# Ordering the neighbour counts of a graph network: permuting matmuls replaced by indirect stores to HBM

## The chip, the cores and the metric

The kernel runs on one core of one Trainium2 chip. The metric is the device time of one launch in microseconds (us). "Batch" below means one of the 32 independent graphs of the input. The engines are called as the profile calls them: PE (TensorE; PEld is its weight load), DVE (VectorE), ACT (ScalarE), POOL (GpSimd) and SP (SyncE, which here only starts transfers).

## The reference

There are 32 graphs of 512 nodes with 64 features. Four graph layers follow each other, and each is `x = layernorm(x + layer(x, adj))`: a normalized product with the adjacency matrix, a Chebyshev filter of order four, a layer of hyperbolic pair distances, and a last layer, the only one that the change touches:

```python
def _dilate_adj(adj, mask):                       # layer 3
    adj_ = jnp.where(eye[None], 1.0, adj)
    nb = (adj_ > 0) & (~eye)[None]
    m = nb.sum(-1)
    rank = jnp.cumsum(nb, axis=-1) - 1            # running count of neighbours in a row
    skip = jnp.where(m > 10, (m + 1) // 2, 1)
    removed = nb & do_dil[..., None] & ((rank + 1) % skip[..., None] == 0)
    rem = removed | jnp.swapaxes(removed, 1, 2)
    return jnp.where(rem, 0.0, adj_)

agg = _weighted_nanquantile_agg(x, adj_d > 0)     # quantiles 0.25, 0.5, 0.75 over each node's neighbours
out = x + agg
y = relu(out @ W1 + b1) @ W2 + b2
```

For each node and each feature the values of the remaining neighbours are sorted, and three quantiles of them are summed with weights.

## The kernel before

The kernel has two paths. The fast one, which runs here, is good for the degrees that such graphs have; a second, `dense_layer3`, runs after it only if a flag says that a degree was out of bounds.

**Lanes.** The fast path does each batch in lanes: `front` (load of the adjacency matrix, its transpose `AT`, layers 0 and 1), `pairs` and `tail` (layer 2), `graph` (which neighbours remain, and in which order), `gather` (the k-th neighbour of every node is fetched by a product of the features with a one-hot matrix), `sort` and `head` (sorting networks of min and max on the fetched values, tiles `SB` and `SH`), and for every pair of batches the dense layer and the store of the result.

**Order.** Nothing runs while it is recorded. Each operation goes through `seq.op` with an engine, a planned duration and its dependences. `Order.issue` then plans all batches at once and writes out one list for each engine, in which lanes of several batches are interleaved; an engine runs its list strictly in that order and waits where an operand is not there. Which ready operation goes next is decided by a due time: a period of 80 planned us times the batch number plus a share, which goes through five knots for each lane (`STAGES`); `STAY` is the advantage that a matmul has on PE if its shape is that of the one before it. Where the plan leaves PE idle for more than 0.3 us, `issue` puts in `stay_active` matmuls (lines 1579 and 1580) whose results nobody reads, one for every 0.11 us.

**The graph lane.** `graph` makes the 0/1 matrix `nbT` of neighbours, counts them, forms running counts with a product of `nbT` and `UC`, marks the removed neighbours in `v`, and puts the remaining ones (with the diagonal) into `V`, 512 x 512, four tiles of 128 rows. ACT writes `V` from PSUM and sums its rows at the same time (`accum_out`), which gives the degrees `m3`, kept in `M3`. `order` ranks the nodes by degree: a key of degree and node number, compared with all keys by ACT (`Sign` with a row sum `sg`), gives the rank `rk`, and `spot`, an integer form of it, is kept for the fetches at the end. Then come the steps that the change replaces:

- `perm`: DVE makes four one-hot tiles of 128 x 512 from the ranks, with the even ranks in the first half of the columns and the odd ones in the second (`iotap`).
- `VP`: 16 matmuls with 512 columns, `V` by `perm`, put the columns of `V` in rank order; ACT copies four tiles.
- `slot`: 10 matmuls with 512 columns, `UC` by `VP`, make the running counts down each column; ACT copies four tiles. `slot` says for each neighbour and each ranked node the place of that neighbour (1, 3, 5, ... for those that are there); the gather lane compares it with constants on DVE to get its one-hot tiles `gather_oh`.
- Four more matmuls, `onesP` by `VP`, give the degrees along the columns, from which `dist` and `OHM` are made.

The pool `gm` holds one buffer for each tag: `perm` takes the buffer of `nbT`, and `VP` that of `v`. The lane `graph` has one PSUM bank.

**The way back.** At the end of a pair of batches the results are stored to `ranked` in HBM by SP and fetched in node order by POOL, four indirect transfers of 32 KB for each batch (`fetch`, line 582, into the tile that the profile calls `tail_x`).

**Helpers.** Most operations are recorded by helpers, so many groups of the profile have one line: `tt` 514, `ts` 518, `stt` 521 and `cp` 524 on DVE, `gtt` 537 and `gts` 541 on POOL, `rsqrt` 813 on POOL, `act` 550, `mm` 569 and `tr` 574 on PE, `dma` 578 on SP. The tile names (`graph_perm`, `pairs_L`) carry the lane.

Of the kernel before, what the change touches and what calls it, by code (L numbers as in the profile page):

```python
# [9 lines left out]
F16 = mybir.dt.float16  # L10
BF16 = mybir.dt.bfloat16
I32 = mybir.dt.int32
# [8 lines left out]
P = 128  # L21
# [218 lines left out]
class Order:  # L240
# [4 lines left out]
    ENGINES = ("PE", "DVE", "ACT", "POOL", "SP")  # L245
    HOP = 0.05
    LATE = 0.08
    STAY = 58.8

    def __init__(self, nc, tc):  # L250
        self.nc, self.tc = nc, tc
# [218 lines left out]
def tile_adj_resnorm(ctx: ExitStack, tc: tile.TileContext, x, adj, nodemask, w1k, b1k, att_w, att_b,  # L470
# [45 lines left out]
    def ts(out, a, s1, s2, op0, op1=None):  # L516
        kw = {} if op1 is None else {"op1": op1}
        vec(lambda: nc.vector.tensor_scalar(out, a, s1, s2, op0=op0, **kw), out, [a], True, (s1, s2))  # L518
# [24 lines left out]
    def act(out, a, f, bias=None, scale=1.0, accum_out=None, after=None):  # L543
        sc = [x for x in (bias, scale) if isinstance(x, bass.AP)]
        kw = {k: v for k, v in (("bias", bias), ("accum_out", accum_out)) if v is not None}
        n = width(out)
        table = "exp" if f in (AF.Ln, AF.Exp) else "sig" if f in (AF.Sigmoid, AF.Tanh) else None
        near = 0.06 if a.space == PSUM else 0.1
        seq.op("ACT", near + n * 0.83e-3 + 0.09 * len(sc) + (0.09 if accum_out is not None else 0.0),
             0.1, lambda: nc.scalar.activation(out, a, f, scale=scale, **kw), [out, accum_out], [a, after] + sc, table)  # L550
# [7 lines left out]
    def mm(out, w, a, start, stop, pair=False, opens=None):  # L558

        n, m = width(a), width(w)  # L560
        if a.dtype == F32:

            t = 0.88e-3 * n if pair else 2 * max(0.9e-3 * m, 0.93e-3 * n)
        else:
            t = max(0.035, n * (0.25e-3 if m == D else 0.455e-3))
        def go():
            if opens is not None:
                seq.open = opens
            return nc.tensor.matmul(out, w, a, start=start, stop=stop)  # L569

        seq.op("PE", t, 0.16, go, [out], [w, a], (64 if w.ap[0][1] <= 64 else 128, 64 if m <= 64 else 128))
# [5 lines left out]
    def dma(out, a):  # L577
        return seq.op("SP", 0.06, 4.0, lambda: nc.sync.dma_start(out, a), [out], [a])

    def fetch(out, rows, at, stored):  # L580

# [202 lines left out]
    bias1 = parts3(b1f, "bias1")  # L784
    xs = dram.tile([B, N, D], F32, name="xs")
    ranked = [dram.tile([N, D], F32, name=f"ranked{b}") for b in range(B)]
    M3 = const.tile([P, B, T], F32, name="M3")

    def diag(a):
# [8 lines left out]
    def col(name):  # L798
        return seq.tile(pools["small"], [P, T], F32, name, 2)
# [96 lines left out]
    def graph(nm, AT, m3, res):  # L896

        gm = pools["gm"]
        nbT = seq.tile(gm, [P, T, N], F16, "nbT", 1)
        ts(nbT, AT, 0.0, None, op0=OP.is_gt)  # L900
        tt(diag(nbT), diag(nbT), identb.unsqueeze(1).to_broadcast([P, T, P]), op=OP.is_gt)
        m = bank()[:, :T]
        for t in range(T):
            for k in range(T):
                mm(m[:, t:t + 1], nbT[:, k, t * P:(t + 1) * P], onesP[:, 0:1], start=(k == 0), stop=(k == T - 1))
        mi = seq.tile(pools["small"], [P, T], I32, "mi", 2)
        ts(mi, m, 1.0, None, op0=OP.add)
# [18 lines left out]
        V = seq.tile(gm, [P, T, N], F16, "V", 1)  # L926
        for t in range(T):
            pt = bank()
            tb = slice(t * P, (t + 1) * P)
            mm(pt, identb, v[:, t, :], start=True, stop=False)  # L930
            for k in range(T):
                kb = slice(k * P, (k + 1) * P)
                mm(pt[:, kb], v[:, k, tb], identb, start=False, stop=False)
                mm(pt[:, kb], nbT[:, k, tb], identb, start=False, stop=(k == T - 1 and t < T - 1))
                if k == t:
                    mm(pt[:, kb], identb, identb, start=False, stop=(t == T - 1))
            act(V[:, t, :], pt, AF.Relu, accum_out=m3[:, t:t + 1])
        res["V"] = V

    def order(b, res):  # L940

        gm = pools["gm"]
        V = res["V"]
        key = col("key")
        stt(key, M3[:, b, :], float(N), iotr, op0=OP.mult, op1=OP.add)
        pt = bank()
        for t in range(T):
            tr(pt[:, t * P:(t + 1) * P], key[:, t:t + 1].to_broadcast([P, P]), identf)
        keyh = col("keyh")
        ts(keyh, key, -0.5, None, op0=OP.add)  # L950
        sg = col("sg")
        for t in range(T):
            junk = seq.tile(gm, [P, N], F16, "junk", 1)
            act(junk, pt, AF.Sign, bias=keyh[:, t:t + 1], scale=-1.0, accum_out=sg[:, t:t + 1])
        rk = col("rk")
# [12 lines left out]
        perm = seq.tile(gm, [P, T, N], F16, "perm", 1, "nbT")  # L968
        for t in range(T):
            ts(perm[:, t, :], iotap, rk[:, t:t + 1], None, op0=OP.is_equal)  # L970
        VP = seq.tile(gm, [P, T, N], F16, "VP", 1, "v")
        for j in range(T):
            pt = bank()
            for t in range(T):
                mm(pt, V[:, t, j * P:(j + 1) * P], perm[:, t, :], start=(t == 0), stop=(t == T - 1))
            act(VP[:, j, :], pt, AF.Copy)
        slot = seq.tile(pools["keep"], [P, T, N], F16, "slot", 2)
        for j in range(T):
            pt = bank()
            for k in range(j + 1):  # L980
                mm(pt, UC[:, :P] if k == j else UC[:, P:2 * P], VP[:, k, :], start=(k == 0), stop=(k == j))
            act(slot[:, j, :], pt, AF.Copy)
        pt = bank()
        for k in range(T):
            mm(pt, onesP, VP[:, k, :], start=(k == 0), stop=(k == T - 1))
        if b % 2 == 0:
            res["ohm"] = OHM[:, b // 2 % 3]
        dist = seq.tile(gm, [P, H2], F16, "dist")
        for i in range(P // HM):
            hm, h = slice(i * HM, (i + 1) * HM), i % 2  # L990
            act(dist[hm], pt[hm, h * H2:(h + 1) * H2], AF.Abs, bias=npart[hm])
# [513 lines left out]
    def within_bounds():  # L1505
# [17 lines left out]
        for i, op in enumerate((OP.is_gt, OP.is_lt)):  # L1523
# [84 lines left out]
    def dense_layer3(iv):  # L1608
# [12 lines left out]
        m3 = keep.tile([P, T], F32, name="m3")  # L1621
        res = {}
        graph(nm, AT, m3, res)
        V = res["V"]
        VT = keep.tile([P, T, N], F16, name="VT")
        for j in range(T):
            pt = bank(F16)
            for t in range(T):
                nc.tensor.transpose(pt[:, t * P:(t + 1) * P], V[:, t, j * P:(j + 1) * P], identb)
            nc.vector.tensor_copy(VT[:, j, :], pt[:, :N])  # L1630
        x3T = keep.tile([D, N], F32, name="x3T")
        pt = bank()
        for t in range(T):
# [197 lines left out]
```

## Time and profile before

| What | Value |
|---|---|
| three runs | 2331.5, 2337.36, 2339.77 us (median 2337.36) |
| profiled execution, its own time | 2326.41 us |
| its span | 2324.6 us |
| granted PE clock, mean | 0.994 |
| busy: PE, DVE, ACT, POOL | 2177.0, 2115.8, 2033.9, 1098.7 us |
| DMA | 57.72 MB, mean 25 GB/s |

The span is the time between the first and the last instruction of the profiled execution; 1.8 us lie around it. A busy time counts the moments in which at least one instruction of the engine, or of the group, was in work, so matmuls that overlap in the pipeline are not counted twice; "mean ns of one" is the length of a single instruction, overlap included. Idle time is put down to the operation that came last before the engine went on.

### The profile page before, as it was taken

To read this page: it belongs to the slowest core of one execution; us is meant where nothing else is said; L and a number is where in the kernel's file an instruction comes from. 1 tells how busy PE (TensorE), PEld (TensorE's weight loads), DVE (VectorE), ACT (ScalarE), POOL (GpSimd) and SP (SyncE) were. 2 spreads that over 40 slices of the span, in tenths; PEclk is the share of its full clock that TensorE was granted. 3 is DMA by queue.
4 is the path that set the end of the run, shared out by engine and by line. 5 is a ranking of instruction groups with operands and counts; after the bars stand their busy time and mean duration, and the time that the engine had idled before them with its cause. 6 is when DMAs were issued, how large, how long until landed. Compare 5 with 4: busy or idle time off the path is not lost. (4 is left out here: it accounts for less than half of the span.)

```text
span 2324.6 us, 53396 instructions
## 1 busy us (share of the span) xinstructions
PE 2177.0 (94%) x18555; PEld 1504.3 (65%) x18555; DVE 2115.8 (91%) x6952; ACT 2033.9 (87%) x5818; POOL 1098.7 (47%) x2256
## 2 busy tenths in 40 slices
PE   6999999999999999999999999999999999999987
PEld 4666666666666666666666666666666666666655
DVE  4556999999999999999999999999999999999996
ACT  6798989999998989898989989898998989899753
POOL 1133445545464544545445554544555454454431
PEclk9999999999999999999999999999999999999999
DMA  1010001111000110100011111001111000100000
GB/s 45 21 42 12 18 22 31 27 28 31 27 18 21 34 28 26 33 26 20 22 31 28 27 33 26 19 21 32 29 27 33 26 19 17 29 15 8 13 15 14
DMA packets 131716, 57.72 MB, mean 25 GB/s; under 512 B 56140, under 2 KB 129516, under 8 KB 131436
## 3 DMA queue, kind: packets, MB, share of 16 engines
q1 hardware_dynamic: 126432, 50.09, 8.0%
q0 software_dynamic: 3840, 3.94, 0.8%
q8 instruction: 148, 2.42, 0.4%
q14 instruction: 132, 1.08, 0.2%
q10 hardware_dynamic: 1164, 0.18, 0.0%
HBM read 41.86 MB, written 12.32 MB: 23 GB/s over the span
## 5 line engine op out<-in xcount | busy, mean ns | idle before, releaser
L514 DVE TENSOR_TENSOR SB<-SB 128x92 f32<-128x92 f32 (+12 forms) x1312 | 555.3, 448 | 15.3 <-ACT SB L550 6.2
L569 PE MATMUL gather_bank<-gather_oh,tail_x3h 128*64 128x256 f16 (+5 forms) x5376 | 496.5, 318 | 7.4 <-ACT SB L550 7.1
L569 PEld LDWEIGHTS <-tail_x3h 128*64 128x64 bf16 x5376 | 333.9, 110 | 134.4 <-issue 26.2
L569 PE MATMUL pairs_bank<-pairs_FT 67*128 67x512 f32 (+7 forms) x768 | 305.6, 504 | 8.5 <-DVE pairs_L L521 2.7
L518 DVE TENSOR_SCALAR gather_oh<-graph_slot 128x256 f16<-128x256 f16 (+9 forms) x864 | 252.7, 343 | 27.1 <-PE gather_bank L569 23.5
L514 DVE TENSOR_TENSOR SH<-SH 128x288 f32<-128x288 f32 (+18 forms) x880 | 271.2, 342 | 3.8
L569 PE MATMUL front_bank<-front_AT,front_y 128*64 128x256 f32 x1536 | 190.4, 385 | 12.3 <-DVE front_y L514 11.5
L569 PEld LDWEIGHTS pairs_bank<-pairs_FT 67*128 67x128 f32 (+1 forms) x768 | 127.7, 190 | 83.8 <-issue 18.2
L582 POOL DMA_INDIRECT tail_x<-ranked,graph_spot x120 | 136.5, 1137 | 74.5 <-issue 41.4
L569 PEld LDWEIGHTS <-graph_nbT 128*128 128x128 f16 x1536 | 117.4, 98 | 78.3 <-issue 34.2
L569 PEld LDWEIGHTS front_bank<-front_AT,front_y 128*64 128x64 f32 x1536 | 108.1, 137 | 78.1 <-DVE front_y L514 22.2
L813 POOL TENSOR_TENSOR front_rs<-front_var,mhalf 128x4 f32<-128x4 f32 x64 | 81.1, 1267 | 131.4 <-DVE front_var L518 120.2
L569 PE MATMUL graph_bank<-graph_perm,graph_V 128*128 128x512 f16 x512 | 137.4, 379 | 5.3 <-DVE graph_perm L518 2.7
L569 PE MATMUL pairs_bank<-FLS,pairs_Wt 128*128 128x66 f32 x1024 | 125.6, 273 | 0.3
L514 DVE TENSOR_TENSOR pairs_RW<-pairs_RW,pairs_EX 128x640 f32<-128x640 f32 x128 | 104.7, 818 | 22.9 <-ACT pairs_EX L550 14.6
L569 PEld LDWEIGHTS pairs_bank<-FLS,pairs_Wt 128*128 128x128 f32 x1024 | 121.0, 192 | 2.5 <-DVE pairs_Wt L521 1.7
L569 PEld LDWEIGHTS <-tabs 128*128 128x128 f16 x1296 | 84.0, 98 | 48.3 <-issue 17.4
L550 ACT ACTIVATE graph_junk<-graph_bank,graph_keyh 128x512 f16<-128x512 f32 x128 | 88.0, 688 | 21.8 <-PE graph_bank L574 18.0
L569 PE MATMUL graph_bank<-UC,graph_nbT 128*128 128x512 f16 (+3 forms) x512 | 97.5, 303 | 8.4 <-ACT graph_v L550 4.1
L550 ACT ACTIVATE SB<-gather_bank 128x448 f32<-128x448 f32 (+7 forms) x288 | 89.3, 359 | 18.2 <-PE gather_bank L569 11.9
L569 PE MATMUL PA<-identf,sort_prod 128*96 128x128 f32 (+3 forms) x576 | 103.0, 282 | 1.5 <-DVE sort_prod L514 1.5
L541 POOL TENSOR_SCALAR tail_uc<-tail_un 128x4 f32<-128x4 f32 x32 | 20.7, 646 | 176.6 <-ACT tail_junk L550 170.9
(374 smaller groups left out, 6469.5 us busy)
## 6 DMA issues: line engine op xcount, KB each, us to landing
front_A<-in_adj_dram SPq DMA_DIRECT2D x128, 256.0 KB, 2.9
front_xr<-in_x_dram SPq DMA_DIRECT2D x32, 128.0 KB, 2.2
xs<-tail_x SPq DMA_DIRECT2D x32, 128.0 KB, 2.1
out_dram<-head_zo SPq DMA_DIRECT2D x31, 128.0 KB, 2.0
ranked<-sort_ap SPq DMA_DIRECT2D x30, 128.0 KB, 1.9
tail_x<-ranked,graph_spot POOLq DMA_INDIRECT x120, 2.5
out_dram<-tail_ends SPq DMA_DIRECT2D x1, 128.0 KB, 1.9
wk<-in_L_gnn_weight_dram ACTq DMA_DIRECT2D x1, 64.0 KB, 3.3
```

The costliest lines, as they stand in the source:

```text
L514: vec(lambda: nc.vector.tensor_tensor(out, a, b, op=op), out, [a, b])
L518: vec(lambda: nc.vector.tensor_scalar(out, a, s1, s2, op0=op0, **kw), out, [a], True, (s1, s2))
L541: gp(lambda: nc.gpsimd.tensor_scalar(out, a, s1, s2, op0=op0, **kw), out, [a] + [x for x in (s1, s2) if isinstance(x, bass.AP)])
L550: 0.1, lambda: nc.scalar.activation(out, a, f, scale=scale, **kw), [out, accum_out], [a, after] + sc, table)
L569: return nc.tensor.matmul(out, w, a, start=start, stop=stop)
L582: seq.op("POOL", 1.15, 2.0, lambda: nc.gpsimd.indirect_dma_start(out, None, rows, bass.IndirectOffsetOnAxis(ap=at, axis=0)), [out], [at], ...
L813: seq.op("POOL", 1.6, 0.5, lambda: nc.gpsimd.tensor_tensor(y, v, mhalf, op=OP.pow), [y], [v])
```

## The change

- **Counts with nodes as rows.** `graph` now makes the matrix transposed, `VT`, without the row sums; the degrees come from 16 matmuls with one column, and DVE copies them to `M3`. The term of `nbT` in that sum becomes four matmuls with 512 columns in place of 16 with 128.
- **Running counts before the ranks.** `order` makes the running counts at once, 16 matmuls `VT` by `UC` (512, 384, 256 and 128 columns, as `nbT` by `UC` in `graph`); ACT copies four tiles of 128 x 512 into `order`, whose row is a node in its own order. POOL writes the degree into two more columns (two `gts`).
- **Stored at their ranks.** DVE makes an integer rank. POOL stores the four tiles with four indirect transfers (`scatter`), each 128 rows of 514 16-bit numbers (1,028 bytes, 131.6 KB in all), each row at its rank in `ordered[b]` in HBM. They are recorded one behind the other; declared independent, they need not wait for each other on the chip.
- **Read back.** SP reads `ordered[b]` in two transfers (even ranks and odd ranks, 263 KB each) into `rows`, which takes the buffer of `v`; `order` takes that of `nbT`.
- **Transposed.** 16 PE transposes of 128 x 128 in 16 bits, two groups of eight, each read by ACT in one copy of 1,024 columns, make `slot`. Four more, of the degree column broadcast to 128, take the place of the product with `onesP`.
- **Gone**: `perm`, `VP`, and the products with `V`, `VP` and `onesP`.
- **Shares.** `STAY` goes from 58.8 to 84.7 and the knots of `STAGES` are others for every lane but `ends` and `check`.

```diff
-    STAY = 58.8
+    STAY = 84.7
...
+    def scatter(rows, at, a, others, ops):
+
+        def go():
+            ins = nc.gpsimd.indirect_dma_start(rows, bass.IndirectOffsetOnAxis(ap=at, axis=0), a, None)
+            for o in others:
+                tc.declare_no_dep(ins.ins, o.ins, reason="ranks of nodes differ")
+            others.append(ins)
+            return ins
+        i = seq.op("POOL", 1.15, 2.5, go, [], [at, a], behind=ops[-1:])
+        ops.append(i)
+        return i
...
+    ordered = [dram.tile([N, N + 2], F16, name=f"ordered{b}") for b in range(B)]
...
             mm(pt, identb, v[:, t, :], start=True, stop=False)
+            mm(pt, identb, nbT[:, t, :], start=False, stop=False)
             for k in range(T):
                 kb = slice(k * P, (k + 1) * P)
-                mm(pt[:, kb], v[:, k, tb], identb, start=False, stop=False)
-                mm(pt[:, kb], nbT[:, k, tb], identb, start=False, stop=(k == T - 1 and t < T - 1))
+                mm(pt[:, kb], v[:, k, tb], identb, start=False, stop=(k == T - 1 and t < T - 1))
                 if k == t:
                     mm(pt[:, kb], identb, identb, start=False, stop=(t == T - 1))
-            act(V[:, t, :], pt, AF.Relu, accum_out=m3[:, t:t + 1])
+            act(VT[:, t, :], pt, AF.Relu)
+        m = bank()[:, :T]
+        for t in range(T):
+            for k in range(T):
+                mm(m[:, t:t + 1], VT[:, k, t * P:(t + 1) * P], onesP[:, 0:1], start=(k == 0), stop=(k == T - 1))
+        cp(m3, m)
...
+        order = seq.tile(gm, [P, T, N + 2], F16, "order", 1, "nbT")
+        for t in range(T):
+            pt = bank()
+            for k in range(T):
+                mm(pt[:, k * P:], VT[:, k, t * P:(t + 1) * P], UC[:, :N - k * P], start=(k == 0), stop=(k == T - 1))
+            act(order[:, t, :N], pt, AF.Copy)
+        for u in range(2):
+            gts(order[:, :, N + u], M3[:, b, :], 1.0, None, op0=OP.mult)
...
+        rank = seq.tile(pools["small"], [P, T], I32, "rank", 2)
+        ts(rank, sg, -0.5, 0.5 * N - 1.0, op0=OP.mult, op1=OP.add)
+        apart, stored = [], []
+        for t in range(T):
+            scatter(ordered[b], rank[:, t:t + 1], order[:, t, :], apart, stored)
...
-        perm = seq.tile(gm, [P, T, N], F16, "perm", 1, "nbT")
-        for t in range(T):
-            ts(perm[:, t, :], iotap, rk[:, t:t + 1], None, op0=OP.is_equal)
-        VP = seq.tile(gm, [P, T, N], F16, "VP", 1, "v")
-        for j in range(T):
-            pt = bank()
-            for t in range(T):
-                mm(pt, V[:, t, j * P:(j + 1) * P], perm[:, t, :], start=(t == 0), stop=(t == T - 1))
-            act(VP[:, j, :], pt, AF.Copy)
+        rows = seq.tile(gm, [P, T, N + 2], F16, "rows", 1, "v")
+        for h in range(2):
+            dma(rows[:, 2 * h:2 * h + 2, :], ordered[b].rearrange("(u p h) n -> h p u n", h=2, u=2)[h], behind=stored)
         slot = seq.tile(pools["keep"], [P, T, N], F16, "slot", 2)
-        for j in range(T):
-            pt = bank()
-            for k in range(j + 1):
-                mm(pt, UC[:, :P] if k == j else UC[:, P:2 * P], VP[:, k, :], start=(k == 0), stop=(k == j))
-            act(slot[:, j, :], pt, AF.Copy)
-        pt = bank()
-        for k in range(T):
-            mm(pt, onesP, VP[:, k, :], start=(k == 0), stop=(k == T - 1))
+        for j in range(0, T, 2):
+            pt = bank(F16)
+            for i in range(2):
+                for c in range(T):
+                    tr(pt[:, i * N + c * P:i * N + (c + 1) * P], rows[:, c, (j + i) * P:(j + i + 1) * P], identb)
+            act(slot[:, j:j + 2, :].rearrange("p j n -> p (j n)"), pt, AF.Copy)
+        pt = bank(F16)
+        for c in range(T):
+            tr(pt[:, c * P:(c + 1) * P], rows[:, c, N:N + 1].to_broadcast([P, P]), identb)
...
-    STAGES = {"front": (-0.67, -0.59, -0.59, -0.4, -0.35), "pairs": (1.01, 1.02, 1.54, 1.44, 1.34),
-              "tail": (2.23, 2.13, 2.56, 2.68, 2.58), "graph": (0.84, 1.06, 1.03, 1.48, 2.2),
-              "gather": (2.92, 2.89, 2.92, 3.03, 2.93), "sort": (4.18, 4.47, 4.53, 5.09, 6.03),
-              "head": (4.54, 5.59, 5.59, 6, 7.54), "ends": (4.04, 4.143, 4.245, 4.348, 4.45),
+    STAGES = {"front": (-0.41, -0.51, -0.53, -0.56, -0.66), "pairs": (0.9, 1.23, 1.43, 1.45, 1.9),
+              "tail": (-1.35, 0.5, 1.73, 2.67, 2.61), "graph": (0.23, 0.59, 0.96, 0.88, 1.02),
+              "gather": (2.61, 2.53, 2.52, 2.42, 2.32), "sort": (4.1, 4, 4.73, 5.42, 5.66),
+              "head": (4.81, 5.68, 5.87, 6.01, 6.9), "ends": (4.04, 4.143, 4.245, 4.348, 4.45),
```

More of the change, by code (lines that the diff above doesn't have):

```diff
@@ L575, in tr, with dma @@
                (128, 64 if width(a) <= 64 else 128))
-    def dma(out, a):
-        return seq.op("SP", 0.06, 4.0, lambda: nc.sync.dma_start(out, a), [out], [a])
+    def dma(out, a, behind=()):
+        return seq.op("SP", 0.06, 4.0, lambda: nc.sync.dma_start(out, a), [out], [a], behind=behind)
+    def scatter(rows, at, a, others, ops):
[8 more added lines that the diff above has]
+        return i
     def fetch(out, rows, at, stored):
@@ L925, in graph @@
             ts(v[:, t, :], v[:, t, :], skip[:, t:t + 1], -1.0, op0=OP.is_equal, op1=OP.mult)
-        V = seq.tile(gm, [P, T, N], F16, "V", 1)
+        VT = seq.tile(gm, [P, T, N], F16, "VT", 1)
         for t in range(T):
@@ L930, in graph @@
             mm(pt, identb, v[:, t, :], start=True, stop=False)
+            mm(pt, identb, nbT[:, t, :], start=False, stop=False)
             for k in range(T):
                 kb = slice(k * P, (k + 1) * P)
-                mm(pt[:, kb], v[:, k, tb], identb, start=False, stop=False)
-                mm(pt[:, kb], nbT[:, k, tb], identb, start=False, stop=(k == T - 1 and t < T - 1))
+                mm(pt[:, kb], v[:, k, tb], identb, start=False, stop=(k == T - 1 and t < T - 1))
                 if k == t:
                     mm(pt[:, kb], identb, identb, start=False, stop=(t == T - 1))
-            act(V[:, t, :], pt, AF.Relu, accum_out=m3[:, t:t + 1])
-        res["V"] = V
+            act(VT[:, t, :], pt, AF.Relu)
[4 more added lines that the diff above has]
+        cp(m3, m)
+        res["VT"] = VT
     def order(b, res):
         gm = pools["gm"]
-        V = res["V"]
+        VT = res["VT"]
+        order = seq.tile(gm, [P, T, N + 2], F16, "order", 1, "nbT")
[6 more added lines that the diff above has]
+            gts(order[:, :, N + u], M3[:, b, :], 1.0, None, op0=OP.mult)
         key = col("key")
@@ L1623, in dense_layer3 @@
         graph(nm, AT, m3, res)
[L1624 to L1630, printed above, removed]
+        VT = res["VT"]
         x3T = keep.tile([D, N], F32, name="x3T")
```

## The prediction

> **What bounds the kernel now.** The chain of work that ended last covers only the last microsecond of this trace (six pieces from 2318.27 us on), so it says nothing of the change. I read the busy times, then the table of stretches, then the waits, then the groups that the change touches.
>
> ```profile
> PE 2177.0 (94%) x18555; PEld 1504.3 (65%) x18555; DVE 2115.8 (91%) x6952; ACT 2033.9 (87%) x5818; POOL 1098.7 (47%) x2256
> ```
>
> PE leads, but 94.4 us of it are the matmuls that nobody reads (79.8 on line 1579, 14.6 on line 1580). Without them PE has 2083 us of work and DVE 2116. The stretches of 58 us say where DVE's idle time lies (columns: PE, PEld, DVE, ACT, POOL busy, clock, DMA share, GB/s):
>
> ```profile
> 0.00:58.00 58.00, 39.71 (x313) 28.01 (x313) 26.83 (x144) 37.23 (x80) 10.30 (x86) 1.00 0.18 45
> ...
> 174.00:232.00 58.00, 57.31 (x455) 39.56 (x452) 39.82 (x127) 49.91 (x139) 21.21 (x51) 1.00 0.04 11
> ...
> 1276.00:1334.00 58.00, 55.12 (x488) 39.34 (x488) 57.13 (x202) 55.09 (x166) 32.85 (x66) 1.00 0.10 27
> ...
> 2204.00:2262.00 58.00, 50.21 (x528) 35.36 (x528) 57.34 (x217) 33.34 (x104) 18.66 (x32) 1.00 0.05 14
> ```
>
> Of DVE's 209 us of idle time, 103 lie before 232 us, where the first batches pass from lane to lane. From 290 us on DVE is busy 52 to 58 of every 58 us, and in the drain, when ACT has run dry, 57.3. So DVE sets the pace, with PE and ACT close behind; the stores `xs` run from 171.1 to 2236.3 us, 31 steps of 66.6 us. What does DVE wait for? The longest entries of its waits between 300 and 2250 us:
>
> ```profile
> DVE pairs_RW L514 <- ACT pairs_EX L550: 13.3, 14, 2.2
> DVE gather_oh L518 <- PE gather_bank L569: 9.2, 14, 2.0
> DVE graph_mi L518 <- PE gather_bank L569: 6.0, 3, 2.0
> ```
>
> They are small and many: no single wait can be removed for a large gain.
>
> **The change, part by part.** The groups it removes, and those that price what it adds:
>
> ```profile
> L518 DVE TENSOR_SCALAR graph_perm<-iotap,graph_rk 128x512 f16<-128x512 f16 x128 | 36.3, 346 | 0.1
> ...
> L569 PE MATMUL graph_bank<-graph_perm,graph_V 128*128 128x512 f16 x512 | 137.4, 379 | 5.3 <-DVE graph_perm L518 2.7 <-ACT graph_VP L550 1.9
> ...
> L569 PE MATMUL graph_bank<-graph_VP,UC 128*128 128x512 f16 x320 | 90.8, 379 | 8.6 <-ACT graph_slot L550 8.0
> ...
> L569 PE MATMUL graph_bank<-UC,graph_nbT 128*128 128x512 f16 (+3 forms) x512 | 97.5, 303 | 8.4 <-ACT graph_v L550 4.1 <-DVE graph_do L521 3.7
> ...
> L550 ACT ACTIVATE graph_slot<-graph_bank 128x512 f16<-128x512 f32 x128 | 76.2, 596 | 6.8 <-PE graph_bank L569 5.1 <-PE gather_bank L569 1.4
> ...
> L550 ACT ACTIVATION_READ_ACCUMULATOR graph_V<-graph_bank 128x1 f32 x128 | 26.6, 208 | 0.0
> ...
> L582 POOL DMA_INDIRECT tail_x<-ranked,graph_spot x120: 940/1021/2002, 397.4 to 2271.0; - x120
> ...
> DMA to landing us min/median/max: 2.3/2.5/4.7
> ```
>
> *DVE.* The 128 `perm` operations go: 36.3 us. Added for each batch are the copy of the degrees and the integer rank, two operations of 128x4; such operations last 0.16 to 0.17 us and start 0.07 to 0.09 us apart where they overlap, so 0.17 to 0.33 us, times 32 is 5.3 to 10.6; I take 5.3, since most stand between others. Sum: **31.0 us less**, all of it on the engine that sets the pace.
>
> *PE.* Where they follow each other, matmuls of 512 columns start 0.217 us apart (four took 1326.80 to 1327.67 us in the timeline) and those of 128 columns with new weights 0.055 apart (1309.68 to 1309.74). Gone are 30 of 512 columns: 6.5 us for each batch. In the sum that makes `VT`, 16 x 0.055 become 4 x 0.217: nothing. Added: `VT` by `UC` at 4 x 0.54 (1304.57 to 1305.11), 2.2 us; 16 matmuls of one column, 0.4 (a like group began at 1364.21, the next at 1364.61); 20 transposes in 16 bits, which the trace doesn't show: between 0.055 each (the V step) and 0.11 (four f32 transposes start 0.44 us before the next group), 1.1 to 2.2, nearer the V step because type and width are its own. Sum: 1.7 to 2.8 us less for each batch, 55 to 91 us. But the built order holds 1164 of the unread matmuls in place of 705, and those outside of the first five batches and the drain go from 49 to 416: 459 x 0.134 us (94.4 / 705) is 61 us that PE is given back. PE thus gets lighter only where it was to stand idle, and a shorter PE is worth nothing on DVE except in its waits for PE.
>
> *ACT.* The row sums go (4 x 0.208), `order` takes the place of `VP` (4 x 0.596 each, nothing), and four copies for `slot` become two of 1,024 columns: 0.596 + 512 x 0.86 ns (slope between the 512- and 256-column copies, 596 and 377 ns) is 1.03, against 2.38 for four of 512, so 0.3 less; at worst twice 0.596 each, nothing less. The built order has four table loads fewer (1.283 each). Sum: 32 x 1.15 + 5, about **42 us less**; on an engine that isn't the bound it gains nothing by itself.
>
> *POOL.* Four stores at the 1.137 us of a fetch (0.94 to 2.0) and two `gts` at 0.49 (group `graph_wrap`): 5.5 us for each batch, 177 in all, 1099 to about 1276 of 2300. It has the room, but its list is in order. In the built order the stores stand among the small operations of `pairs` and `tail`: between `tail_uc` and `tail_al` POOL has 14.0 us of work before and 20.5 after. DVE waited for POOL 1.4 us in all in the steady part, so this lane has cover; without it 6.5 us in each batch.
>
> *The trip through HBM.* A store of 131.6 KB lies between a fetch of 32 KB (2.5 us to landing, 4.7 at most) and a load of 256 KB (2.9); I take 2.9, bounds 1.9 (the fastest kind, SP's `ranked`) to 4.7. The reads are 263 KB each: 2.9. The path from the last `Sign` to the first `slot` copy is then rank 0.17, first to last store 13.1 us of POOL's list on average, landing 2.9, read 2.9, eight transposes 0.5: 19.6 us. Between the two, ACT's list holds 21.8 us of other work on average (14.0 to 28.2), 25 us of time at its 87%. So the trip is hidden, by about 5 us, in the mean and not in every batch. If it isn't, the transposes hold up PE's list, and with it everything.
>
> *SP.* The two reads wait on SP for the stores, mostly behind the load of `xr` and ahead of the next loads of `A` and stores of results. SP stood 552.6 us waiting for buffers to come free (76 times, for `front_A`), so the queue has slack; the cover is those waits. Other cost: 33.7 MB more traffic beside 57.7 at 25 GB/s, nothing at a DMA share of 0.1.
>
> *Shares.* Depth hardly changes: by DVE work in list order (the trace's durations), the first `SB` operation comes after 128 us in place of 129, and what follows the last operation on the last batch's adjacency shrinks by some 16 of 183. I take no gain at the ends.
>
> *A rule against the change.* POOL's 120 indirect transfers took 0.94 to 2.0 us beside a DVE that was over 90% busy, so I price a store at 1.137. The Trainium skill, page "SBUF — State Buffer", section "SBUF: two separate sides", says that a transfer issued from GpSimd starves while DVE holds the port they share: about 620 ns alone, about 3100 ns beside a DVE copy. By that page my estimate would be four stores at 3.1 us, 7.9 us more on a path with 5 us of slack: slower by over 60 us net. The 2.0 us maximum here doesn't show it.
>
> *Sum.* On the profiled execution: 2326.4 - 31.0 with DVE's idle time unchanged = 2295.4. The median of the runs stands 1.0047 above that execution (2337.36 / 2326.41): **2306 us**.
>
> **The rivals.** *PE's relief reaches DVE too* (0.17). DVE's waits for `gather_bank` (23.5 us for `gather_oh` over the whole span, 6.0 for `graph_mi`) shrink, since PE's list is shorter; worth up to 25: 2270 profiled, 2281 as a median. Against it: the unread matmuls refill PE.
>
> *The trip through HBM comes late* (0.25; slower). For it: stores spread over 13 us in a list that itself waits for ACT and DVE (`tail_th` on ACT's tanh, 70.7 us in 29 waits), and batches whose ACT cover is only 14 us. Each us of mean lateness costs 32. It outweighs the gain beyond 31 / 32 = 1.0 us and is measurably slower beyond 1.2; at 1.5 it gives 2295.4 + 48 = 2343 profiled, 2354 as a median. Against it: cover of 25 for 19.6.
>
> *Nothing moves* (0.08). DVE's saved 31 us turn into waits because ACT and PE hold the period: within 7 us of 2337.
>
> **How the numbers follow.** The forecast (DVE's saving, idle time as before) has 0.50, its own range 2290 to 2328. Faster: 0.50 + 0.17; same 0.08; slower 0.25. About 0.3% (7 us) is what a measurement of this kernel can tell from no change. The range goes down to 2270, past the first rival's 2281 with the full PE relief, and up to 2362, lateness 1.75 us; beyond lie some 0.17.
>
> **What would show it.** Right: DVE busy near 2085, ACT near 1992, POOL near 1276, PE near 2120 to 2180; `perm` gone, stores near 1.1 us with a landing near 3, no long wait of PE or of `slot` for `rows`. Wrong: PE waiting for the transfer into `rows`, stores over 2 us, POOL's small operations late so that DVE waits for POOL by more than some 30 us, or DVE's idle time over 240.

## The result: 9.4% slower, and the profile after

| | before | after |
|---|---|---|
| median | 2337.15 us (2331.5 to 2339.77, 4 runs) | 2555.39 us (2549.93 to 2560.14, 4 runs) |
| ratio, 95% interval | 1 | 1.0943 [1.0913, 1.0973] |
| profiled execution: own time, span | 2326.41, 2324.6 us | 2554.85, 2553.1 us |
| granted PE clock, mean | 0.994 | 0.992 |
| DVE idle (span less busy) | 208.8 us | 443.4 us |

The prediction, 2306 us with a range to 2362, was wrong. The busy times of the page of after:

```profile
PE 2447.9 (96%) x19314; PEld 1754.5 (69%) x19334; DVE 2109.7 (83%) x6888; ACT 2040.6 (80%) x5622; POOL 1169.3 (46%) x2448
```

DVE, ACT and POOL have about the work they had. PE has 271 us more, in a change that takes products away from it. PE is now the bound: the chain of work that ended last covers the whole span in this trace, and PE holds two thirds of it.

```profile
PE 66%; DVE 21%; ACT 9%; issue 2%; POOL 1%; DMA 0%; POOLq 0%; ACTq 0%; DVEq 0%
```

Which products? The groups of after (busy us, mean ns of one, idle before them):

```profile
L569 PE MATMUL gather_bank<-gather_oh,tail_x3h 128*64 128x448 f16 (+5 forms) x5376 | 758.0, 316 | 1.8 <-ACT SB L550 0.7
L518 DVE TENSOR_SCALAR gather_oh<-graph_slot 128x256 f16<-128x256 f16 (+9 forms) x864 | 260.7, 346 | 169.6 <-PE gather_bank L569 168.3
L569 PE MATMUL front_bank<-front_AT,front_y 128*64 128x256 f32 x1536 | 272.0, 384 | 4.3 <-DVE front_y L514 1.6
L583 POOL DMA_INDIRECT ordered<-graph_order,graph_rank x128 | 157.6, 1231 | 93.2 <-DVE graph_rk L518 54.7
...
L1605 PE MATMUL PA<-zero 128*128 128x256 bf16 x970 | 135.5, 278 | 0.1
```

The first and third rows are matmuls that the diff does not touch: the gather products and the products with `AT`. The same three rows in the page of before:

```profile
L569 PE MATMUL gather_bank<-gather_oh,tail_x3h 128*64 128x256 f16 (+5 forms) x5376 | 496.5, 318 | 7.4 <-ACT SB L550 7.1
L518 DVE TENSOR_SCALAR gather_oh<-graph_slot 128x256 f16<-128x256 f16 (+9 forms) x864 | 252.7, 343 | 27.1 <-PE gather_bank L569 23.5
L569 PE MATMUL front_bank<-front_AT,front_y 128*64 128x256 f32 x1536 | 190.4, 385 | 12.3 <-DVE front_y L514 11.5
```

Count and length of one are unchanged; the busy time of the two groups of matmuls is up by 261.5 and 81.6 us. (The last row of after, with 25.8 us on line 1606, is the matmuls that nobody reads: 161.3 us for 94.4 before.) A busy time that grows at equal count and equal length can only mean that the instructions overlap less. The second row is the bill: DVE, which waited 23.5 us for `gather_bank`, waits 168.3.

The timelines show the overlap (start, length, a run of like instructions). First after, then before, one run of the 448-column gather products each:

```profile
1318.21 4.00 PE L569 MATMUL gather_bank<-gather_oh,tail_x3h 128*64 128x448 f16 x24
```

```profile
1344.84 1.87 PE L569 MATMUL gather_bank<-gather_oh,tail_x3h 128*64 128x448 f16 x18
```

After: 24 in 4.00 us, 0.167 us of the run for each. Before: 18 in 1.87 us, 0.104 for each. These are lengths of whole runs. The starts of the single products say it more exactly: before, they come in pairs, 0.007 us apart within a pair and 0.189 us from pair to pair, so 0.095 us for each; after, they come one by one, 0.189 us apart (1318.42 to 1319.74 us), twice as much. "128*64" in these rows says that a matmul uses 64 of the 128 columns of the array. The code issues every such product twice, for the two halves of the nodes, into the two column halves (`for h in range(2)` around `mm`, output partitions `h * D` to `(h + 1) * D`). Where a matmul in one half is followed by one in the other, the two run side by side; where it is followed by one in the same half, they queue. The run of after holds twelve products of one half and then twelve of the other; where the two chains meet, the first products of the second start before the last of the first, which brings the mean of the run down to 0.167.

The built orders differ in just that. Of the 5376 gather products, 4140 follow a product of the other half before, and 199 after; of 1024 front products (1536 records in the page), 889 and 128. After holds 281 runs of exactly twelve gather products in one half with nothing between them.

Where that comes from is in the diff, in the lines on the shares. An operation's due time goes through five knots along the depth of its lane. The knots of `gather` used to be nearly level (between 2.89 and 3.03) and now fall from 2.61 to 2.32, and those of `front` used to rise and now fall from -0.41 to -0.66. With falling knots, the deeper an operation lies, the earlier it is due: once the first product of a chain of one half has run, its second is due before the first of the other half, so one chain is finished before the other begins. The planner does not mind, since its duration for a product of 64 columns (`0.25e-3` per column) is that of one in a pair, in whatever order it stands.

### The profile page after: what moved, and what is told of

Same layout as the page of the kernel before. It is cut to its first block, busy times and chain, and to the rows that moved or that the text cites. A ratio compares the mean times of both kernels' runs of the same rounds, so it can differ in the third digit from the quotient of the medians.

```text
span 2553.1 us, 55271 instructions
## 1 busy us (share of the span) xinstructions
PE 2447.9 (96%) x19314; PEld 1754.5 (69%) x19334; DVE 2109.7 (83%) x6888; ACT 2040.6 (80%) x5622; POOL 1169.3 (46%) x2448
## 4 chain that ended last, share of the span: by engine, by line
PE 66%; DVE 21%; ACT 9%; issue 2%; POOL 1%; DMA 0%; POOLq 0%; ACTq 0%; DVEq 0%
PE gather_bank L569 28%; PE front_bank L569 12%; PE pairs_bank L569 9%; DVE SB L514 6%; PE graph_bank L569 4%; PE front_bank L574 3%; DVE pairs_Q L514 3%; PE head_bank L569 2%; PE pairs_bank L574 2%; DVE pairs_L L521 2%; DVE SH L514 2%; PE PA L569 2%; PE graph_bank L574 2%; PE PA L1605 1%; ACT graph_v L550 1%
## 5 line engine op out<-in xcount | busy, mean ns | idle before, releaser
L569 PE MATMUL gather_bank<-gather_oh,tail_x3h 128*64 128x448 f16 (+5 forms) x5376 | 758.0, 316 | 1.8 <-ACT SB L550 0.7
L569 PEld LDWEIGHTS <-tail_x3h 128*64 128x64 bf16 x5376 | 498.4, 110 | 207.8 <-issue 16.8
L518 DVE TENSOR_SCALAR gather_oh<-graph_slot 128x256 f16<-128x256 f16 (+9 forms) x864 | 260.7, 346 | 169.6 <-PE gather_bank L569 168.3
L569 PE MATMUL front_bank<-front_AT,front_y 128*64 128x256 f32 x1536 | 272.0, 384 | 4.3 <-DVE front_y L514 1.6
L569 PEld LDWEIGHTS front_bank<-front_AT,front_y 128*64 128x64 f32 x1536 | 169.5, 137 | 74.5 <-issue 8.5
L583 POOL DMA_INDIRECT ordered<-graph_order,graph_rank x128 | 157.6, 1231 | 93.2 <-DVE graph_rk L518 54.7
L1306 POOL MEMSET SB<- 128x10 f32 (+2 forms) x96 | 17.2, 182 | 318.3 <-DVE sort_prod L514 196.9
L1605 PE MATMUL PA<-zero 128*128 128x256 bf16 x970 | 135.5, 278 | 0.1
L550 ACT ACTIVATE front_uT<-front_bank 128x256 f32<-128x256 f32 x128 | 48.8, 381 | 92.7 <-PE front_bank L569 92.3
L569 PEld LDWEIGHTS <-graph_nbT 128*128 128x128 f16 x1024 | 63.9, 97 | 73.5 <-issue 42.7
L1605 PEld LDWEIGHTS <-zero 128*128 128x128 bf16 x970 | 94.1, 100 | 16.2 <-issue 4.9
```

What stands on the lines that cost most here:

```text
L583: ins = nc.gpsimd.indirect_dma_start(rows, bass.IndirectOffsetOnAxis(ap=at, axis=0), a, None)
L1306: seq.op("POOL", 0.1, 0.06, lambda d=d: nc.gpsimd.memset(d, PAD), [d], [])
L1605: return nc.tensor.matmul(PA[:, 2 * P:], zero[:, :P], zero, start=False, stop=False)
```

## The experiments

Every run was compared with runs of the kernel before on the same chip; these had a median of 2330.21 us for the first four kernels, 2364.22 for the next four and 2363.25 for the last four, so only ratios go from one group to another.

### Shares or graph lane?

The theory: the shares pulled the column halves apart, and that is the loss. The rival: the graph lane itself, whose rows come late from HBM.

*Only the graph lane* (`STAGES` and `STAY` of the kernel before in the changed kernel):

```diff
-    STAY = 84.7
+    STAY = 58.8
...
-              "gather": (2.61, 2.53, 2.52, 2.42, 2.32), "sort": (4.1, 4, 4.73, 5.42, 5.66),
+              "gather": (2.92, 2.89, 2.92, 3.03, 2.93), "sort": (4.18, 4.47, 4.53, 5.09, 6.03),
```

> The change with the old numbers for STAGES and STAY: the new graph lane, the stores and the reads are all there, only the plan is weighted as before. In its built order the matmuls of gather and front that fill one half of the columns each (64 wide) change from one half to the other 4115 of 5376 and 893 of 1024 times, as in the kernel before (4140 and 889); in the changed kernel only 199 and 128 times. Theory (the new shares broke the alternation of the two column halves, and a pair in different halves runs at once): the gather matmuls fall from 758 us busy to about 500, those of front with front_y from 272 to about 190, and the time is what the prediction had for the change alone, 2306 us (2285 to 2335). Rival 1 (the trip through HBM on POOL and SP, with its waits, is the cost): 2500 to 2560 us. Rival 2 (the new shares are bad because of the order of the lanes, not of the halves): 2285 to 2335 too, so this run does not tell it from the theory.

Measured: 2408.53 us, 1.0346 [1.0297, 1.0395]. The halves alternate again (4115 of 5376), the gather group is back at 515.5 us and the front group at 190.4, and almost two thirds of the loss are gone. The expected gain did not come. Part of what is left may be that the new lane is late under shares that were not made for it: the stores stood on POOL for `graph_rk` for 103.9 us (54.7 in after), one took 4988 ns, and POOL holds 11% of the chain. PE also ran at half clock for 103 us, against 26 before. How the 3.5% divide between these was not tested.

*Only the shares* (the kernel before with those of the change):

> The kernel before with the new numbers for STAGES and STAY and nothing else: perm, VP and the products are there, no stores. In its built order the halves change 210 and 128 times. Theory: gather matmuls near 758 us busy and front_y near 272, PE has the full old graph lane as well, so slower than the changed kernel or near it: 2550 to 2650 us. Rival 1 (trip through HBM): near 2337 us, at most 2380. Rival 2 (order of the lanes): 2500 to 2650 us, as the theory.

Measured: 2589.64 us, 1.1111 [1.1086, 1.1136], with the old graph lane. The gather group takes 763.2 us and the front group 271.8, as in after; 210 and 128 changes of half. The loss needs nothing of the graph lane; under these shares the lane even takes 1.7% off (1.1111 to 1.0943).

*Only the second half moved.* The knots of before, but every product into the second half is due 40 planned us later; no other edit:

```diff
+        if self.second:
+            self.late[i] = self.second
...
-            key.append(period * (b + knots[k] + (knots[k + 1] - knots[k]) * (x - k)))
+            key.append(period * (b + knots[k] + (knots[k + 1] - knots[k]) * (x - k)) + self.late.get(i, 0.0))
...
                         for h in range(2):
+                            seq.second = 40.0 * h
                             mm(pt[h * D:(h + 1) * D, o:o + w], x3h[:, q, j, :], oh[:, j, h, :w],
...
```

> The kernel before, with its own shares and graph lane; only the matmuls of gather and front that go into the second column half are due 40 planned us later, so that one half runs before the other: the halves change 120 of 5376 and 77 of 1024 times in place of 4140 and 889. Theory (alternation of the halves is what the changed shares lost): gather matmuls near 760 us busy, and 2500 to 2600 us. If the shares cost by something else: under 2400 us.

Measured: 2612.25 us, 1.1058 [1.1038, 1.1078]. Its gather group (120 changes of half):

```profile
L572 PE MATMUL gather_bank<-gather_oh,tail_x3h 128*64 128x448 f16 (+5 forms) x5376 | 823.2, 316 | 3.2 <-ACT SB L553 1.5
```

Old lane, old knots, the same work: pulling the halves apart is enough to lose 10.6%. The edit also makes half of the products later, but PE is not waiting: it is busy for 2537.2 of 2608.9 us, against 2177.0 before. The next section asks the reverse, whether joining the halves takes the loss away while everything else in the change stays.

### The halves joined

If the halves belong together, record them together: one operation of the planner that issues both matmuls.

```diff
+    def mm2(whole, outs, w, moving, start, stop):
+        n = width(moving[0])
+        t = (0.88e-3 if moving[0].dtype == F32 else 0.25e-3) * n
+        def go():
+            return [nc.tensor.matmul(o, w, a, start=start, stop=stop) for o, a in zip(outs, moving)]
+        seq.op("PE", 2 * t, 0.16, go, [whole], [w] + moving, (128, 64))
...
-                        for h in range(2):
-                            mm(pt[h * D:(h + 1) * D, o:o + w], x3h[:, q, j, :], oh[:, j, h, :w],
-                               start=(j == 0 and q == 0), stop=(i < len(pieces) - 1 and j == T - 1 and q == 2))
+                        mm2(pt[:, o:o + w], [pt[h * D:(h + 1) * D, o:o + w] for h in range(2)], x3h[:, q, j, :],
+                            [oh[:, j, h, :w] for h in range(2)],
+                            start=(j == 0 and q == 0), stop=(i < len(pieces) - 1 and j == T - 1 and q == 2))
```

*In the changed kernel:*

> The changed kernel with its new shares, only that the two matmuls of one weight into the two column halves (gather, and the products with AT in front) are recorded as one operation, so that they stand one behind the other: the halves change 5135 of 5376 and 896 of 1024 times. Same matmuls, same planned cost. Theory: gather matmuls at or below 500 us busy, front_y near 190, and the time falls to about 2300 us (2270 to 2335). Rival 1 (trip through HBM): stays at 2500 to 2560. Rival 2 (order of the lanes): stays at 2480 to 2560, since the order of everything else is kept as nearly as the plan allows.

Measured: 2368.65 us, 1.0163 [1.0136, 1.0191]; 5135 changes of half, the gather group at 454.5 us, below its 496.5 of before. The new lane and the new shares are still there, so neither the trip through HBM nor the order of the lanes is the main cause. *In the kernel before:*

> The kernel before with the same joining of the two halves and its own shares: the halves change 5123 times in place of 4140 in gather, 890 in place of 889 in front. Theory: the gather matmuls, 496.5 us busy before, lose the quarter that ran alone: 400 to 450 us. DVE sets the pace there and waited 23.5 us for the gather bank in all, so the time gains 0 to 30 us: 2305 to 2337, most likely 2325. Rivals 1 and 2: 2337 us, no change.

Measured: 2359.29 us, 1.0126 [1.0076, 1.0175]; the gather group at 458.3 us. So 7.8 of the 9.4% come back, which together with the run of the halves moved apart settles the main cause. But both times lie above the expected ones: a gather group that is lighter by some 40 us does not make the kernel faster, in either version.

One possible reason is visible in the second of these. In stretches of 4 us (PE, PEld, DVE, ACT, POOL busy, clock, DMA share, GB/s):

```profile
886.00:890.00 4.00, 2.57 (x40) 2.20 (x35) 3.53 (x15) 3.95 (x15) 1.27 (x2) 0.99 0.12 28
890.00:894.00 4.00, 4.00 (x21) 3.50 (x21) 3.13 (x24) 2.56 (x13) 1.10 (x1) 0.50 0.02 5
894.00:898.00 4.00, 4.00 (x14) 2.21 (x13) 2.12 (x10) 1.81 (x8) 1.03 (x1) 0.50 0.14 33
...
906.00:910.00 4.00, 4.00 (x36) 2.72 (x33) 2.72 (x6) 3.67 (x9) 1.53 (x8) 0.87 0.24 72
```

PE has 1.4 us of idle time in one stretch, and then runs at half its clock for some 17 us, in which DVE gets 2.1 to 3.1 us of work done out of each 4. Summed over the trace, the time at half clock is 104 us in 13 events of 3.4 to 17.1 us, against 26 us in 5 before. Between 300 and 2250 us DVE works 0.61 of the time in stretches of 4 us with a clock of at most 0.75, and 0.96 in the others. By these, 78 us more at half clock would cost 78 x (0.96 - 0.61) / 0.96, about 28 us: an estimate, near the 29 us that the kernel lost. (The Trainium skill, page "TensorE: Matmul & The Clock Gate", section "What's actually happening", has the same two states, half clock after an idle window of about 3.4 us and full clock after a busy one; the rows here show the drop after less idle time than that within a stretch of 4 us, and a return only after about 17.)

*Is the clock all of it?* Then more unread matmuls in PE's idle time should bring the time back. In both joined kernels, the changed one first and then the one before:

```diff
-                for _ in range(int((t - spare - fill) / 0.11)):
+                for _ in range(int((t - spare - fill) / 0.08)):
...
-        seq.issue(80.0, STAGES, stay_active, 0.3)
+        seq.issue(80.0, STAGES, stay_active, 0.0)
```

> e3 (changed kernel, halves joined) with more unread matmuls: one for every 0.08 planned us that PE stands idle, from the first on, in place of one for every 0.11 beyond 0.3; 3389 in place of 1293, about 2100 x 0.11 = 230 us more of PE work that nobody needs. Rival 3 (the granted clock is what e3 lacks): clock back to 0.992 or more, and in spite of the extra work faster than e3, 2310 to 2355 us. Theory with the trip as the remaining cost, or without the clock: no gain, 2365 to 2420 us, since PE only has more to do.

> e4 (kernel before, halves joined, 2359 us at clock 0.978) with the same filling: 2016 unread matmuls in place of 731. Rival 3: clock 0.992 or more, 2310 to 2340 us. Without the clock as a cause: 2355 to 2400 us.

Measured: 2432.0 us, 1.0288 [1.027, 1.0307], and 2413.84 us, 1.0221 [1.0202, 1.024]. The clock did come back in the first (19 us at half clock in place of 80) and in part in the second (51 in place of 104), and the time got worse: in the first, PE is busy for 2354.5 us, 512.9 of them unread matmuls, and DVE's wait for `gather_bank` rises from 41.4 to 54.4 us. Filling is no remedy at this density; it costs more than the clock gives back. How much of the loss of the joined kernels is the clock's is not shown.

*The old graph lane with the new shares and the halves joined*, to price the lane alone:

> The kernel before with the new shares and with the two halves joined: against e3 (2369 us, the same but for the graph lane) it shows what the new graph lane itself is worth under the same shares. Theory (the graph lane saves 31 us of DVE and some 90 of PE, but the trip is hidden): e8 slower than e3 by 0 to 30 us, 2370 to 2400. Rival 1 (trip through HBM late): e8 faster than e3, 2330 to 2360. Rival 3 (a lighter PE stands idle and its granted clock falls to half for some 17 us each time): e8 has fewer planned gaps (823 unread matmuls against 1293), so a clock above the 0.983 of e3 and 2330 to 2365.

Measured: 2394.05 us, 1.0139 [1.0117, 1.0162], against 1.0163 for the same with the new lane. The two stand on different chips and their intervals overlap: no gain of the lane is seen here. Nor does half clock take 17 us each time, as the third rival has it: the 16 events of this trace last 3.4 to 6.8 us. The next pair, on one chip, asks again for the price of the lane.

### The knots turned round

The smallest remedy: the same ten numbers, rising.

```diff
-    STAGES = {"front": (-0.41, -0.51, -0.53, -0.56, -0.66), ...
+    STAGES = {"front": (-0.66, -0.56, -0.53, -0.51, -0.41), ...
...
-              "gather": (2.61, 2.53, 2.52, 2.42, 2.32), ...
+              "gather": (2.32, 2.42, 2.52, 2.53, 2.61), ...
```

*In the changed kernel, and with the old graph lane under the same shares:*

> The changed kernel with the same ten numbers for front and gather, in rising order in place of falling; no other edit. Theory (the falling knots pulled the two column halves apart, and that is the whole loss): the halves alternate again (5049 of 5376 in the built order), the group gather_bank<-gather_oh,tail_x3h is back near 500 us, front_bank<-front_AT,front_y near 190, DVE's wait for gather_bank below 50, and what the lane saves shows: 0.98 to 1.00 of the kernel before. Rival (the new lane and the other shares cost something by themselves, as the 1.6% of the kernel with joined halves suggests): 1.01 to 1.03.

> The kernel before with exactly the shares of e10_reversed (old graph lane, new shares with rising knots). Against e10_reversed it prices the new lane alone, under the same shares and with the halves alternating in both. Theory (the lane's 31 us of DVE work show in the time): e10_reversed is 25 to 35 us faster than this one, which stands at 1.00 to 1.015 of the kernel before. Rival (DVE's saved work turns into waits, as between e3_halves and e8_new_shares_halves, 1.0163 and 1.0139 of the kernel before): within 8 us of each other.

Measured: 2398.18 us, 1.0137 [1.0112, 1.0162], and 2426.9 us, 1.027 [1.025, 1.0291]. Two rows of the first:

```profile
L569 PE MATMUL gather_bank<-gather_oh,tail_x3h 128*64 128x448 f16 (+5 forms) x5376 | 485.8, 321 | 23.8 <-ACT SB L550 14.5
L518 DVE TENSOR_SCALAR gather_oh<-graph_slot 128x256 f16<-128x256 f16 (+9 forms) x864 | 255.3, 344 | 49.9 <-PE gather_bank L569 42.7
```

Turning ten numbers round takes the loss from 9.4 to 1.4%, as joining the halves took it to 1.6%: some 8% of the time was the order of the halves. The 1.4% lie in the range of the rival, not in that of the theory. The pair also prices the graph lane: **28.7 us faster** under equal shares (single runs differ by 21 to 41 us), with DVE busy for 2104.3 against 2128.7 us. The prediction's term was 31.0.

What is left, 2.7% with the old lane, belongs to the rest of the new shares. DVE's longest waits from 300 to 2250 us in that kernel:

```profile
DVE gather_oh L518 <- PE gather_bank L569: 33.2, 22, 4.8
DVE front_y L514 <- ACT front_R L550: 18.7, 10, 3.2
DVE graph_v L518 <- ACT graph_v L550: 16.0, 17, 2.7
```

Before, the same list began with 13.3 and 9.2 us. The waits are longer and still spread over many places, and DVE works 0.93 of the time at full clock where it worked 0.96; half clock takes 86 us against 26. Which lane's knots are to blame was not tried.

### A planner that knows the price

The last pair changes the planner's cost: a product of 64 columns counts 1.6 times (0.167 / 0.104) if the one before it on PE was not of the other half. (By the starts given above the price is 2.0; in the two orders built with 1.6 no product directly follows one of its own half.) The knots of all lanes but `ends` and `check`, and `STAY`, were then fitted anew to that planner's own span, separately for the new and the old graph lane.

```diff
                 issue += 0.0 if tab == shape else 0.09
+                if self.half[i] is not None and half in (None, self.half[i]):
+                    issue *= 1.6
+                half = self.half[i]
```

> The changed kernel with a planner that charges a matmul of 64 columns 1.6 times its duration when the one before it on PE is not of the other half (0.167 against 0.104 us, as measured), and with knots fitted to that planner. Theory (the lane is a gain once the shares know what a lost pair costs): 0.95 to 0.985 of the kernel before. Rival (no gain is left in the lane): 0.995 or more.

> The kernel before with the same corrected planner and knots fitted to it in the same manner: tells how much of e12_fitted is the fit and how much the lane. Theory: 0.97 to 1.00 of the kernel before, and e12_fitted 25 to 45 us faster than it. Rival (the gain is the fit's alone): the two within 10 us.

Measured: 2352.68 us, 0.9957 [0.9939, 0.9975], with the new lane, and 2381.2 us, 1.0077 [1.0057, 1.0097], with the old one; one more run of the latter took 5318.43 us and is left out, and why it took so long is not known. The first is ahead of both kernels of the change, by 0.4%, with an interval that ends just below 1, and by about 9% (0.9957 / 1.0943 = 0.910):

```profile
PE 2121.4 (90%) x18902; PEld 1499.7 (64%) x18931; DVE 2107.6 (89%) x6888; ACT 2024.9 (86%) x5626; POOL 1186.2 (50%) x2448
```

The two differ by 28.5 us, the lane with its own fit against the old lane with its own. It is the fit that falls short of the shares of before: the old lane with the fitted knots is 0.8% slower than with its own. Its planner does not know the half clock, of which the faster kernel shows 137 us in 30 events, though DVE works 0.91 of the time there, so it loses little by it; most of DVE's idle time lies at full clock, where it works 0.95. Why the ratio stayed above the expected 0.985 was not followed further; the trace shows no single long wait for it.

## Why the prediction was wrong, step by step

**The step that failed is "Shares".** It read the new knots for the depth of the pipeline alone, found the ends nearly unchanged, and took nothing. In its place stands, put in us of the last chip (2363.25): the falling knots of `gather` and `front`, after against turned round, 1.0943 - 1.0137 = 0.081, **190 us**; the rest of the shares, 1.027 - 1, **64 us**; the graph lane, **-29 us** (the after is scaled from its own chip). They make up the 9.4% by the way they are taken, each the step from one kernel to the next, so their sum is no test of them, and other steps would give other parts: under the falling knots the lane takes off 1.7%. The knots were in the diff, and the built order, which the prediction used for the stores and the filling, would have shown 199 changes of half for 4140. None of the rivals had the shares as its mechanism.

A rule that spoke against this was there to be weighed. The Trainium skill, page "TensorE: Matmul & The Clock Gate", section "Why this matters for your kernels", says that matmuls with few output rows run side by side if each lands in a column group of its own; 0.095 us for one product in alternating halves and 0.189 in the same half are that rule as this kernel shows it.

**DVE's term** was nearly right as work: `perm` gone (37.8 us in the kernel with the old lane and turned knots), the copy of the degrees 4.9 and the rank 5.2 added, so -27.7; the prediction took half of the added 10.1 as hidden. In after itself it doesn't show: DVE is busy for 2109.7 us and not 2085, since the old lane under the new shares already takes 2136.7. Of the signs of being wrong that the prediction named, one came, DVE's idle time, 443.4 us for a limit of 240. Under the turned knots the lane gave -28.7 us, so a saving on DVE can become time, as the forecast had it. That the sizes agree is in part luck: with joined halves the lane gave nothing (1.0163 against 1.0139), and under the shares of before it cost 3.5%.

**The trip through HBM** held (its time was about as sized), and the rival that it comes late fell. In after, by source line and tile:

```profile
L583 POOL DMA_INDIRECT ordered<-graph_order,graph_rank x128: 1036/1126/2490, 71.7 to 2429.7; - x128
...
DMA to landing us min/median/max: 2.6/3.0/4.4
```

```profile
L578 SPq DMA_DIRECT2D graph_rows<-ordered x64: 359/459/1607, 85.8 to 2434.7; - x64
...
  ACT graph_slot L550: 17.0, 18
  ACT graph_dist L550: 6.6, 16
...
DMA to landing us min/median/max: 2.7/3.1/4.2
```

Stores and reads land in 3.0 and 3.1 us (median; 2.9 was taken for both), and the two waits of ACT come to 23.6 us on an engine that had slack; PE waited 0.2 us on the rows. With the knots turned round, PE and PEld waited less than 4 us for them in all.

**The rule on starved GpSimd transfers**, for which the prediction cites the Trainium skill, page "SBUF — State Buffer", section "SBUF: two separate sides" (3.1 us beside a DVE copy), is not what the stores show. They took 1036 to 2490 ns, mean 1231, beside a DVE that is 83% busy; single ones took up to 4988 ns in the kernel with the old shares. Which of DVE's operations ran beside each store is not shown. The prediction's choice of 1.137 was 8% low, that of the page 2.5 times too high for the mean.

**POOL** was sized well: stores 158.4 and the two `gts` 26.3 us, 184.7 in the kernel with turned knots, for 177; in after POOL is busy for only 1169.3 of the 1276 us forecast, as its other work takes less under the new shares (980.7 us with the old lane). **PE's** relief was there too, in that pair: 2221.3 to 2175.3 us although the unread matmuls rose from 134.7 to 166.1, about 77 us of work less, within the 55 to 91. **ACT**: the copies and row sums of the lane went from 258.6 to 218.6 us, 40.0 less for 36.8 predicted, and the 1,024-column copy took 1.017 us for 1.03. The engine's busy time fell by only 10.6 us, as other groups grew; whether it bought any time is not separated.

## What to carry to other kernels

A busy time that rises while count and mean length stay the same is lost overlap: look at the timeline for what ran side by side before, and at the order for what came between. When a change brings a new order, price the order itself, not only the operations: which instructions are fast only next to a certain other one, and does the thing that writes the order know it? And test parts under equal schedules: here the lane gained 29 us under equal shares in one pair and nothing in another, and the shares that came with it hid that behind 250.

## What was not expected of the hardware

- Two matmuls of 64 columns in different column halves, one right after the other, take 0.095 us each at 448 columns; in the same half 0.189. Where a chain of twelve in one half meets a chain of twelve in the other, the records show the first three products of the second starting before the last of the first (1319.75 to 1320.31 us). With nearly all in one half the gather group took 758.0 to 823.2 us for 454.5 to 515.5.
- An idle PE is not always free even where it isn't the bound: 1.4 us of it in 4 was followed by 17.1 us at half clock, in which DVE worked less (0.61 for 0.96 busy over all such stretches). In that kernel (before, halves joined) the events last 3.4, 6.8, 10.2 or 17.1 us, but for the last, and PE was idle for 0.9 to 3.4 us of the 3.4 before each. Idle time alone does not decide: of 24 stretches of 3.4 us at full clock with at least 1.2 us of it, 11 were followed by half clock. How much it costs depends on what DVE has in hand: 0.91 for 0.95 in the fitted kernel.
- The same kernel before took 2330.21, 2364.22 and 2363.25 us in three groups of runs on different chips, 1.5% apart, more than some of the effects sought here.
